# A 3x3 convolution by transformed tiles: three sums per image group on GpSimd in place of VectorE

## The chip, the cores and the metric

The kernel runs on one core of a Trainium2 chip. A core has TensorE (PE in the profile, with PEld for its weight loads), which multiplies matrices and writes to PSUM; VectorE (DVE) and ScalarE (ACT), which work element by element on SBUF and PSUM; GpSimd (POOL), which can also work element by element on SBUF and issues some of the transfers; and SyncE (SP), which here only issues transfers. Each engine runs its own queue in order, and engines wait for each other by semaphores. The metric is device time in microseconds.

## The reference

Two bottleneck layers, one after the other, on 64 images of 1024 channels, 14 x 14 pixels, all in fp32. A layer is:

```python
out = relu(_bn(_conv(x,   w1, b1, 1, 0)))     # 1x1, 1024 -> 256
out = relu(_bn(_conv(out, w2, b2, 1, 1)))     # 3x3, 256 -> 256
out =      _bn(_conv(out, w3, b3, 1, 0))      # 1x1, 256 -> 1024
x   = relu(x + softplus(residual_scale) * out)
```

The batch norm `_bn` takes mean and variance of each channel over the batch itself, so a stage has to have ended before the next can be normalised. The change lies in the 3x3 convolution, which runs once in each layer.

## The kernel before

The 256-channel activation of all 64 images, `y_all`, stays in SBUF: 128 partitions, two slots of channels (`MS` = 2), 12544 pixels. The stages are the first 1x1 convolution (to about 309 us of the profiled span), the 3x3 convolution of layer 0 (`conv2`, to about 560), the statistics and the fused third and first convolutions of the two layers (to about 1310), the 3x3 convolution of layer 1 (to about 1565) and the last stage.

`conv2` works on eight groups of eight images (`NG` = 8, `GI` = 8), in place: a group's rows in `y_all` are read, and its results are put down in the same rows. In the direction of the rows it computes four output rows from six transformed products (`NF` = 6), in the direction of the columns even and odd columns from four filters (`NK` = 4). The six products of a group come in three pairs, (1, 2), (3, 4) and (5, 0).

- **Inputs.** For each pair, VectorE forms combinations of rows (`combine`: the tiles `steps` and `r`, by `stt`, a scalar_tensor_tensor at L593, and by additions at L682, L688 and L699), then sums, differences and steps of columns (`sums` L624, `v` L630, `diffs` L640). ScalarE makes edges (L635, L636, L590, L714 to L716).
- **Products.** For each of the six, TensorE multiplies `sums` into the bank `m`, `diffs` into `l`, and `v` into the banks `columns` (two buffers). ScalarE copies `m` into `columns` ahead of the last (L758, L760) and `l`, with both signs, into `ls` in SBUF (L768). A product with 224 columns of moving data has 32 multiplications; products 3 and 4 have 168, since the last tile of rows doesn't need them.
- **Outputs.** VectorE adds `columns` and `ls` into `f` (L801), once for each product; `f` has three buffers. The generator `finish` then puts a group together. From products 1 and 2 come `a` = their sum (tile `fa`, L829) and `d` = their difference (tile `fb`, L830); from 3 and 4 `c` (tile `fc`, L835) and `e` (L836). Output rows 1 and 2 are `d` + 2`e` and `a` + 4`c` (four L593). Output row 0 is `a` + `c` (L843) plus product 0. Output row 3 is `d` + 8`e` (L593, in place in `fb`) plus product 5 (L859); the last row of an image, which has only `d` and product 5, is L860.
- **Row 0's product 0.** In groups 0 to 5 (`by_transfer`) it is added by two transfers that accumulate in SBUF, issued by GpSimd (L871). Groups 6 and 7 add it on VectorE (L846, L873, L879). Group 7 (`last_group`) also takes statistics of its rows on VectorE as it writes them.

While a group runs, ScalarE normalises the next group and takes the moments of the one before (`long_work`, `moment`, `norm`), by long instructions over 1568 elements.

The order of the program decides TensorE's order, and some of VectorE's and ScalarE's (`keep_in_program_order`). A scheduler may permute the rest of VectorE's, ScalarE's and GpSimd's instructions by its own estimates, and places the waits. GpSimd has nothing in `conv2` but the transfers of L871 and, at the end, a few instructions on two numbers each (`merge`).

Of the kernel before, what the change touches and what calls it, by code (L numbers as in the profile page):

```python
# [87 lines left out]
def bottlenecks(ctx: ExitStack, tc: tile.TileContext, x, w1s, w2s, w3s, pars, out):  # L88
    nc = tc.nc
# [466 lines left out]
    def conv2(psum, pool, b, par, aff, affine_of, stats):  # L556
# [14 lines left out]
        full = RT - 1  # L571
# [12 lines left out]
        def new(tag, tiles=RT):  # L584
            v = pool.tile([P, MS * RT * LINE], FP, tag=tag, name=tag, bufs=BUFS.get(tag, 1))
            return v[:, : MS * tiles * LINE].rearrange("p (s r l) -> p s r l", s=MS, r=tiles)
# [5 lines left out]
        def stt(to, a, by, c):  # L592
            return nc.vector.scalar_tensor_tensor(to, a, by, c, ALU.mult, ALU.add)  # L593
# [210 lines left out]
        def halves(f):  # L804

            return f.rearrange("p o r (i q c) -> p q (o r i) c", i=GI, q=2)

        def outputs(c):
            return c.add_to(new("f", c.lines // GI))

        def finish():


            for g in range(NG):
                out_rows = [y_grp[:, :, g, k::4, :] for k in range(4)]
                last_group = g == NG - 1

                by_transfer = g < NG - 2

                def stat(k, lines):  # L820
                    if last_group:
                        for o in range(MS):
                            nc.vector.bn_stats(stats[:, o, 1 + k, :], lines[o])

                ca = yield
                fa = outputs(ca)
                fb = outputs((yield))
                a, d = new("fa"), new("fb")
                nc.vector.tensor_add(a, fa, fb)  # L829
                nc.vector.tensor_sub(d, fa, fb)  # L830

                fa = outputs((yield))
                fb = outputs((yield))
                c, e = new("fc", full), fa
                nc.vector.tensor_add(c, fa, fb)  # L835
                nc.vector.tensor_sub(e, fa, fb)  # L836
                a3, d3 = (v[:, :, :full] for v in (a, d))
                for o in range(MS):
                    stt(out_rows[1][:, o, :full], e[:, o], 2.0, d3[:, o])
                    stt(out_rows[2][:, o], c[:, o], 4.0, a3[:, o])  # L840
                if by_transfer:

                    nc.vector.tensor_add(out_rows[0][:, :, :full], a3, c)  # L843
                    nc.scalar.activation(out_rows[0][:, :, full], a[:, :, full], AF.Copy)
                else:
                    nc.vector.tensor_add(a3, a3, c)  # L846
                stt(d3, e, 8.0, d3)
                if g == 0:
                    begin(out_rows[1][:, :, :full])
                if last_group:  # L850
                    for o in range(MS):
                        lines = y_grp[:, o, g, 1 : 1 + 4 * full].rearrange("p (r k) l -> p r k l", k=4)[:, :, :2]
                        for k in range(2):
                            moment(lines, idle[:, : 2 * full * LINE].rearrange("p (r k l) -> p r k l", k=2, l=LINE), o, k, g)

                fa = outputs((yield))

                end = y_grp[:, :, g, H - 1]
                nc.vector.tensor_add(out_rows[3], d3, fa[:, :, :full])  # L859
                nc.vector.tensor_add(end, d[:, :, full], fa[:, :, full])  # L860
                stat(0, [out_rows[3][:, o] for o in range(MS)])
                stat(1, [end[:, o] for o in range(MS)])
                if last_group:
                    merge()

                cb = yield
                if by_transfer:

                    f = outputs(cb)
                    for o in range(MS):  # L870
                        nc.gpsimd.dma_start(out=out_rows[0][:, o], in_=f[:, o], accum_op=ALU.add)  # L871
                    continue
                nc.vector.tensor_add(halves(a), halves(a), cb.by_columns(cb.ls))  # L873
                for j, q in enumerate((EVEN, ODD)):
                    for o in range(MS):
                        to, more = (
                            v[:, o].rearrange("p r (i q c) -> p q r i c", i=GI, q=2)[:, q] for v in (out_rows[0], a)
                        )
                        nc.vector.tensor_add(to, cb.banks[:, q, o].rearrange("p (r i c) -> p r i c", r=RT, c=WH), more)  # L879
                    stat(2 + j, [out_rows[0][:, o].rearrange("p r (i q c) -> p q r i c", i=GI, q=2)[:, q] for o in range(MS)])  # L880
            yield
# [8 lines left out]
        def begin(lines):  # L890

            mv = small.tile([P, MS, nc.vector.BN_AGGR_DIM], FP, tag="mv_first", name="mv_first")
            for o in range(MS):
                nc.vector.bn_stats(first_stats[:, o], lines[:, o])
            for o in range(MS):
                nc.vector.bn_aggr(mv[:, o, :], first_stats[:, o])
            nc.vector.tensor_scalar(center, mv[:, :, 0], -1.0, None, ALU.mult)

        def moment(y, to, o, k, g):
            act(to, y, (AF.Identity, AF.Square)[k], bias=center[:, o : o + 1], accum_out=moments[:, o, k, g : g + 1])  # L900

        def merge():

            n = GPX * (NG - 1) + 2 * full * LINE
            m = small.tile([P, MS, 2], FP, tag="m12", name="m12")
            for o in range(MS):
                nc.vector.tensor_reduce(m[:, o], moments[:, o], mybir.AxisListType.X, ALU.add)
            eng = nc.gpsimd
            eng.tensor_scalar(m, m, 1.0 / n, None, ALU.mult)
            var = small.tile([P, MS], FP, tag="m12var", name="m12var")  # L910
            eng.tensor_tensor(var, m[:, :, 0], m[:, :, 0], ALU.mult)
            eng.tensor_sub(var, m[:, :, 1], var)
            eng.tensor_sub(m[:, :, 0], m[:, :, 0], center)

            for half in range(2):
                to = stats[:, :, 0, 3 * half : 3 * half + 3]
                eng.memset(to[:, :, 0], n / 2)
                eng.tensor_copy(to[:, :, 1], m[:, :, 0])
                eng.tensor_scalar(to[:, :, 2], var, n / 2, None, ALU.mult)
# [26 lines left out]


        made, finished = items(), finish()
        next(finished)
        queue = [next(made) for i in range(3)]  # L950
# [498 lines left out]
```

## Time and profile before

| | us |
|---|---|
| median of 3 runs | 1959.82 (1959.64 to 1960.51) |
| the profiled execution, its own time | 1959.24 |
| its span in the profile | 1957.5 |
| VectorE busy in the span | 1552.4 |
| TensorE busy in the span | 1919.9 |
| GpSimd busy in the span | 532.0 |
| L843, 12 instructions, each | 0.85 |
| L859, 16 instructions, each | 0.85 |
| L860, 16 instructions, each | 0.38 |

A line of a timeline gives start and duration in us from the start of the span, engine, source line, operation, the tiles written and read, the shape, and in brackets how long the engine had idled before it and what ended that. Tile names are those of the program without buffer numbers. Durations of successive instructions of an engine overlap a little, so the time that one takes from its engine is better read from start to start. Many matmuls have one source line, L168, which is that of a helper; they are told apart by tile. In the page's first part PE is TensorE at work on matmuls, whose ends are modelled.

### The profile page before, as it was taken

The numbers are of one execution on the slowest core, as the hardware profiler recorded it, in microseconds if no ns is written. First come the engines' busy times: TensorE is split into PE (matmuls) and PEld (weight loads), VectorE is DVE, ScalarE is ACT, GpSimd is POOL, SyncE is SP. The second block draws the span as 40 slices with busy tenths as digits, with TensorE's granted clock in tenths as the row PEclk, the third lists the DMA queues.
The fourth block names the chain that finished last, engine by engine and source line by source line (L and its number), as shares of the span: only waits on it lengthen the run. The fifth ranks groups of instructions, "written<-read, shape, count | busy, mean of one in ns | idle before, by whom it ended". The sixth has DMA issues, their size and how long they took to land.

```text
span 1957.5 us, 26989 instructions
## 1 busy us (share of the span) xinstructions
PE 1919.9 (98%) x9430; PEld 1614.4 (82%) x9430; DVE 1552.4 (79%) x2491; ACT 1041.5 (53%) x2082; POOL 532.0 (27%) x638
## 2 busy tenths in 40 slices
PE   9999999999999999999999999989999999999998
PEld 5555558999997799999999999989999887555554
DVE  5778768999998667676776776699999976888786
ACT  2222214677775055555555555457777641666665
POOL 0111100000105133433433333301010051666664
PEclk9999999999999999999999999999999999999999
DMA  7766635576747634444444444257667386899997
GB/s 289 278 248 254 249 112 165 178 208 191 207 142 203 198 135 187 173 165 177 182 169 165 179 184 166 99 183 204 203 192 207 124 199 232 298 322 339 336 341 264
DMA packets 188983, 408.39 MB, mean 209 GB/s; under 512 B 24944, under 2 KB 165136, under 8 KB 172336
## 3 DMA queue, kind: packets, MB, share of 16 engines
q1 hardware_dynamic: 161728, 324.66, 48.5%
q0 software_dynamic: 21504, 30.94, 6.9%
q10 hardware_dynamic: 5616, 51.06, 6.3%
q8 instruction: 75, 1.23, 0.3%
q14 instruction: 60, 0.49, 0.1%
HBM read 263.75 MB, written 115.34 MB: 194 GB/s over the span
## 4 chain that ended last, share of the span: by engine, by line
PE 90%; DVE 7%; issue 1%; ACT 1%; DMA 1%; SPq 0%; POOL 0%; DVEq 0%
PE ay L168 17%; PE cy L168 16%; PE columns L168 13%; PE cp L168 12%; PE ap L168 10%; PE m L168 6%; PE l L168 6%; PE ax L168 4%; PE cx L168 4%; PE ps L168 1%; DVE x L466 1%; DVE ct L431 1%; DVE f L801 0%; DMA home<-y 0%; DVE ct L433 0%
## 5 line engine op out<-in xcount | busy, mean ns | idle before, releaser
L333 ACT ACTIVATE cu<-cy,scale 128x196 f32<-128x196 f32 (+1 forms) x552 | 257.7, 473 | 286.7 <-PE cy L168 279.6
L168 PE MATMUL columns<-v,ub 128*128 128x224 f32 (+1 forms) x1536 | 301.1, 337 | 0.7 <-ACT columns L760 0.7
L168 PEld LDWEIGHTS columns<-v,ub 128*128 128x128 f32 x1536 | 269.4, 188 | 4.1 <-ACT columns L760 1.2
L333 ACT ACTIVATE x<-x,shift 128x392 f32<-128x392 f32 x428 | 239.7, 613 | 55.1 <-POOL x L492 53.2
L466 DVE SCALAR_TENSOR_TENSOR x<-cp,scale,x 128x196 f32<-128x196 f32 (+1 forms) x368 | 178.1, 484 | 98.0 <-PE cp L168 96.4
L168 PE MATMUL cy<-ct,ws 128*128 128x196 f32 (+1 forms) x736 | 222.0, 383 | 1.1 <-ACT cu L333 1.1
L168 PE MATMUL ay<-at,ws 128*128 128x196 f32 (+1 forms) x752 | 209.2, 381 | 0.0
L487 POOL TENSOR_TENSOR x<-x,cu 128x196 f32<-128x196 f32 (+1 forms) x184 | 159.2, 865 | 174.1 <-ACT cu L333 162.5
L492 POOL TENSOR_TENSOR x<-x,cu 128x392 f32<-128x392 f32 x124 | 125.9, 1015 | 192.8 <-DVE x L466 188.1
L168 PEld LDWEIGHTS ay<-at,ws 128*128 128x128 f32 x752 | 136.4, 190 | 33.6 <-ACT au L333 0.5
L168 PEld LDWEIGHTS cy<-ct,ws 128*128 128x128 f32 x736 | 133.4, 190 | 36.4 <-ACT cu L333 3.8
L168 PE MATMUL m<-sums,ua 128*128 128x224 f32 (+1 forms) x752 | 147.6, 340 | 6.2 <-DVE sums L624 6.2
L168 PE MATMUL l<-diffs,ub 128*128 128x224 f32 (+1 forms) x768 | 149.7, 338 | 3.0 <-PE columns L168 2.9
L513 POOL TENSOR_TENSOR x<-x,cu 128x392 f32<-128x392 f32 x120 | 124.5, 1038 | 86.1 <-DVE x L466 79.2
L871 POOL DMA_DIRECT2D y<-f x24 | 31.1, 1532 | 412.8 <-DVE f L801 320.8
L168 PEld LDWEIGHTS l<-diffs,ub 128*128 128x128 f32 x768 | 133.6, 189 | 7.0 <-PE columns L168 5.9
L168 PEld LDWEIGHTS m<-sums,ua 128*128 128x128 f32 x752 | 132.2, 191 | 8.7 <-DVE sums L624 7.9
L466 DVE SCALAR_TENSOR_TENSOR x<-cx,scale,x 128x196 f32<-128x196 f32 (+1 forms) x184 | 89.3, 485 | 59.1 <-PE cx L168 58.2
L333 ACT ACTIVATE au<-ay 128x196 f32<-128x196 f32 (+1 forms) x141 | 53.6, 380 | 152.0 <-PE ay L168 149.3
L168 PE MATMUL cx<-y,w 128*128 128x196 f32 (+1 forms) x404 | 124.1, 392 | 0.4 <-DVE x L1130 0.4
L168 PE MATMUL cy<-y,w 128*128 128x196 f32 (+1 forms) x404 | 123.8, 392 | 0.0
L168 PE MATMUL cp<-zt 128*128 128x257 f32 x392 | 118.8, 385 | 1.8 <-DVE zt L1030 1.7
(211 smaller groups left out, 3950.1 us busy)
## 6 DMA issues: line engine op xcount, KB each, us to landing
x<-in_x SPq DMA_DIRECT2D x62, 1568.0 KB, 6.8
ub<-u SPq DMA_DIRECT2D x94, 768.0 KB, 5.0
x<-mid SPq DMA_DIRECT2D x32, 1568.0 KB, 8.6
mid<-x ACTq DMA_DIRECT2D x31, 1568.0 KB, 5.1
out<-x SPq DMA_DIRECT2D x123, 392.0 KB, 6.5
ua<-u SPq DMA_DIRECT2D x94, 256.0 KB, 3.0
u<-y POOLq DMA_DIRECT2D x48, 256.0 KB, 5.9
home<-y SPq DMA_DIRECT2D x90, 96.0 KB, 4.2
```

The lines of the kernel that those rows point to most:

```text
L168: tc.keep_in_program_order(nc.tensor.matmul(*args, **kw))
L333: tc.keep_in_program_order(nc.scalar.activation(*args, **kw))
L431: nc.vector.tensor_add(t2, t3, ys[0][0])
L466: nc.vector.scalar_tensor_tensor(v, bank, self.scale[:, o : o + 1], v, ALU.mult, ALU.add)
L487: nc.gpsimd.tensor_add(self.part(1, 1), self.part(1, 1), u3)
L492: nc.gpsimd.tensor_add(v, v, self.u12)
L513: nc.gpsimd.tensor_add(v, v, self.u12[:, i * self.n : (i + 1) * self.n])
L871: nc.gpsimd.dma_start(out=out_rows[0][:, o], in_=f[:, o], accum_op=ALU.add)
```

## The change

Three sums of `finish` are issued on GpSimd: the last step of output row 0 that isn't a transfer (`a` + `c`, groups 0 to 5), and the sum that puts down output row 3 with the last row of each image (groups 0 to 6). Group 7 keeps its sums on VectorE. Values and places are the same. In each of the two 3x3 convolutions GpSimd gets 6 + 7 + 7 instructions, which VectorE loses. From the second hunk on, line numbers of the changed kernel are higher by one: L859 and L860 become L860 and L861, L871 becomes L872.

```diff
@@ -840,7 +840,7 @@
                     stt(out_rows[2][:, o], c[:, o], 4.0, a3[:, o])
                 if by_transfer:
 
-                    nc.vector.tensor_add(out_rows[0][:, :, :full], a3, c)
+                    nc.gpsimd.tensor_add(out_rows[0][:, :, :full], a3, c)
                     nc.scalar.activation(out_rows[0][:, :, full], a[:, :, full], AF.Copy)
                 else:
                     nc.vector.tensor_add(a3, a3, c)
@@ -856,8 +856,9 @@
                 fa = outputs((yield))
 
                 end = y_grp[:, :, g, H - 1]
-                nc.vector.tensor_add(out_rows[3], d3, fa[:, :, :full])
-                nc.vector.tensor_add(end, d[:, :, full], fa[:, :, full])
+                eng = nc.vector if last_group else nc.gpsimd
+                eng.tensor_add(out_rows[3], d3, fa[:, :, :full])
+                eng.tensor_add(end, d[:, :, full], fa[:, :, full])
                 stat(0, [out_rows[3][:, o] for o in range(MS)])
                 stat(1, [end[:, o] for o in range(MS)])
                 if last_group:
```

## The prediction

> **What bounds the kernel now.** I began with the page's first two parts, to see which engines are full and where.
>
> ```profile
> span 1957.5 us, 26989 instructions
> PE 1919.9 (98%) x9430; PEld 1614.4 (82%) x9430; DVE 1552.4 (79%) x2491; ACT 1041.5 (53%) x2082; POOL 532.0 (27%) x638
> ```
>
> TensorE is busy over the whole span, but the change touches only the two 3x3 convolutions, about 309 to 559 us and 1316 to 1563 us. So I read two image groups there (columns: stretch, length, busy time and instructions of PE, PEld, DVE, ACT and POOL, then clock, DMA).
>
> ```profile
> 418.42:452.50 34.08, 33.76 (x193) 33.23 (x193) 33.43 (x37) 24.99 (x49) 2.55 (x2) 1.00 0.70 198
> 452.50:486.60 34.10, 33.77 (x192) 33.27 (x193) 33.45 (x37) 25.06 (x49) 2.56 (x2) 1.00 0.68 197
> ```
>
> Here VectorE is as full as TensorE: 33.4 of 34.1 us against 33.8. Which sets the pace is told by who waits. From 384 to 520 us, VectorE's one listed wait is for ScalarE, never for TensorE; TensorE pauses once a group.
>
> ```profile
> DVE r L593 <- ACT r L715: 1.2, 4, 0.3
> ...
> PE l L168 <- PE columns L168: 0.6, 2, 0.3
> ```
>
> ```profile
> 416.57 1.54 PE columns L168 x8
> 418.11 0.31 issue
> 418.42 1.75 PE l L168 x8
> ```
>
> The second fence is the chain that ended last. The l product reads diffs (L640), which VectorE wrote from 417.24 to 418.32 us; the product starts at 418.42. So in a group VectorE sets the pace, and TensorE follows with only 0.3 us of its own idle time. The timeline of VectorE gives what is to move, and its neighbours:
>
> ```profile
> 414.70 0.85 DVE L843 TENSOR_TENSOR y<-fa,fc 128x672 f32<-128x672 f32 x1
> 415.47 0.85 DVE L593 SCALAR_TENSOR_TENSOR fb<-f,fb 128x672 f32<-128x672 f32 x1
> 416.24 1.08 DVE L801 TENSOR_TENSOR f<-columns,ls 128x896 f32<-128x896 f32 x1
> 417.24 1.08 DVE L640 TENSOR_TENSOR diffs<-r 128x896 f32<-128x896 f32 x1
> 418.24 0.85 DVE L859 TENSOR_TENSOR y<-fb,f 128x672 f32<-128x672 f32 x1
> 419.01 0.38 DVE L860 TENSOR_TENSOR y<-fb,f 128x224 f32<-128x224 f32 x1
> 419.31 2.95 DVE L699 TENSOR_TENSOR steps<-y 128x2688 f32<-128x2688 f32 x1
> ```
>
> Instructions overlap by 0.08 us, so by start to start L843 costs 0.77 us, L859 0.77 and L860 0.30: 1.84 us a group.
>
> **What the Trainium skill says.** "SBUF — State Buffer", Who interferes with whom: a VectorE instruction with two SBUF inputs contends with a GpSimd instruction that reads SBUF, and the later one "fully blocks"; one with at most one SBUF input, outside the two-port modes, does not contend. The trace agrees, in both directions. A GpSimd add of 128x196 takes 0.60 us alone and 1.35 us behind an L418:
>
> ```profile
> 804.06 0.97 DVE L418 TENSOR_TENSOR at<-x,at 128x784 f32<-128x784 f32 x1 [1.24 <-PE ay L168]
> ```
>
> ```profile
> 802.27 0.60 POOL L487 TENSOR_TENSOR x<-x,cu 128x196 f32<-128x196 f32 x1
> ...
> 804.14 1.35 POOL L487 TENSOR_TENSOR x<-x,cu 128x196 f32<-128x196 f32 x1 [1.27 <-ACT cu L333]
> ```
>
> The page says that issue order decides who blocks, not what happens when VectorE has an unbroken queue. The timeline near 1674 us has that case:
>
> ```profile
> 1673.89 0.64 DVE L522 TENSOR_SCALAR x<-x,shift 128x392 f32<-128x392 f32 x1
> 1674.45 1.37 DVE L430 TENSOR_TENSOR ct<-y 128x392 f32<-128x392 f32 x1
> ```
>
> ```profile
> 1674.28 1.13 POOL L487 TENSOR_TENSOR x<-x,cu 128x392 f32<-128x392 f32 x1
> ```
>
> The GpSimd add arrives while L522 runs, and L430 follows L522 without a gap. The add goes first, 0.11 us over its usual 1.02, and L430 takes 1.37 us; subtractions of its shape that meet no add take 0.55. So a waiting GpSimd gets the port ahead of VectorE's next instruction. "GPSIMD Engine Reference", Performance versus the Vector engine, gives 4497 ns for a 2048-element add, an estimate of 2.2 ns an element. The trace: 0.60 us for 196 and 1.015 for 392 (L492), so 2.13 ns an element and 0.18 fixed.
>
> **The change, part by part.** Between 0.60 and 1.015 us the line gives GpSimd 1.61 us for 672 elements and 0.66 for 224; 3.9 us a group on an engine busy 2.55 of 34 would be nothing, were it not for the port.
>
> *One block.* Behind L418, which ended at 805.03, the 196-element add ended at 805.49: 0.46 us later. With 476 more elements an add ends 0.46 + 1.01 = 1.47 us after the instruction that held it up. A blocked VectorE instruction ends 0.43 us after the add (L430: 1675.83 against 1675.40), 0.12 less than its free 0.55; unblocked it would start 0.08 before its predecessor's end. So VectorE loses 1.47 - 0.12 + 0.08 = 1.43 us to a 672-element add, and 0.48 to one of 224 (with 28 more elements, 0.06).
>
> *Where they fall.* In the changed program's order, for groups 2 to 5: L835, L640, L836, four L593 (y), L593 (fb), L801, L699, L593, L801. L843's add needs L835, so it asks while L640 runs, and goes before L836: -0.77 + 1.43. L859's needs the first of these L801, so it asks in the 2.95 us of L699, and goes before the next L593: -0.77 + 1.43. L860's comes behind that L593, beside an L801, which reads PSUM: 0.48 hidden, -0.30; without that cover +0.48. Sum: 2.86 - 1.84 = +1.02 us.
>
> *Reordering.* All of TensorE's and SyncE's instructions keep their order; the scheduler permutes some of VectorE's and ScalarE's. An L801 now stands before the L593 that waited 0.30 us for L715, so that wait is covered: -0.30. L640 before L836 brings diffs early, so the pause at l goes, but the pace is VectorE's. A group: +0.72.
>
> *Other groups.* Group 1 has other neighbours (L630, L640, L699) but the same sum. In group 0 L860 has no cover, +1.50, but there VectorE idles 1.35 us for TensorE before an L801 (at 350.96), so +0.15. Group 6 moves only L859 and L860: four L880, which read PSUM, cover 1.2 us of the first; some 0.25 + 0.48 - 1.07 = -0.35. Group 7 keeps its place. A convolution: 0.15 + 5 x 0.72 - 0.35 = 3.4; two: +6.8 us.
>
> *The rest.* The two transfers of L871 stand behind L859 and L860 on GpSimd, but wait as before for the later L801 (DVE f L801), by whose end both adds are done: nothing. They landed in 6.5 us, and ScalarE reads the rows some 12 us after issue; a delay over 2.5 us would hold up its copies for L801. L801 gets a wait on GpSimd for f's buffer, 14 us after the add was ready to go: nothing. VectorE's L801, late by up to 1.9 us within a group, runs 1.5 to 4 us after TensorE has finished its banks, so the delay does not come back round.
>
> The profiled execution took 1959.24 us, 1.74 around its span; 1957.5 + 6.8 + 1.7 = 1966.0, and as the median lies 0.6 above it, 1966.6.
>
> **Rivals.**
> *Worse packing.* L860 is never covered (+0.48) and the 0.30 us wait stays: a group costs 1.50, ten of them 15, with group 0 at 0.6 and group 6 at 0: +16, 1976. For it: the adds write and read in rows of 112, and every shift of an add against VectorE breaks a cover. Against: the order puts an L801 there.
> *VectorE keeps the port.* If its next instruction wins, an add runs only beside L801 (1.0 us of cover, 0.43 left): -1.84 + 0.86 = -1.0 a group. TensorE then limits: its pause of 0.31 us, 0.33 with start-up of the stalled product, in 14 groups is worth 4.6. By the chain's own pieces its work is less still: four products of 6.08 us (m and l 1.51 each, two columns 1.53 each) and two of 4.58 (1.14, 1.14, 1.15, 1.15) make 33.5 a group, 0.55 under 34.05, which is 7.7. Between them, 1954, faster. It decides once an add costs VectorE less than half of (1.84 + 0.30), 1.07 us. Against it: L430 above; all 13 of its instructions that meet an add there take 1.37.
> *Nothing to measure.* One of the two big adds, asking later than I put it, meets an L801: 1.43 + 0.43 - 2.14 = -0.28 a group, ten of them -2.8, and groups 0 and 6 about nothing: 1957.
>
> **How the numbers follow.** Blocks as costed or somewhat less or more, about 1962 to 1972: 0.48; worse packing, 1972 to 1982: 0.20; nothing to measure, 1956 to 1962: 0.14; VectorE keeps the port: 0.18. This kernel's measurement tells 0.2%, 3.9 us. Of the first case a tenth lies within that. So faster 0.19, same 0.17, slower 0.64. The likeliest time is 1966.6, its own range 1962 to 1972. Leaving out a tenth at either end of all cases: 1954.5 to 1977.
>
> **What would show it.** Right: L836 and the L593 behind L699 near 2.2 us where 0.85 stood, GpSimd's adds stretched by the L640 and L699 before them, groups of 34.8 us, TensorE with more pauses. Wrong: VectorE's durations unchanged and adds of many microseconds (VectorE keeps the port), or groups of 33.7 us. It is also wrong if GpSimd's late adds hold L871, and through it ScalarE, or if TensorE was the pace after all, so that VectorE can lose 0.7 us a group unseen.

## The result: 0.43% slower

| | before | changed |
|---|---|---|
| median, us | 1959.82 (1958.33 to 1960.51, 5 runs) | 1968.33 (1966.97 to 1968.77, 5 runs) |
| the profiled execution, own time / span | 1959.24 / 1957.5 | 1966.97 / 1965.2 |
| first 3x3 convolution, first to last `columns` product | 282.4 | 286.1 |
| second, likewise | 281.7 | 286.4 |
| one group in the middle (L829 to the next L829) | 34.07 | 35.21 |

The ratio of the medians is 1.0043, with a 95% interval of 1.0029 to 1.0056. The two convolutions are 3.7 and 4.6 us longer, 8.3 together; the span is 7.7 longer, so all of it is there. (The text before the result put them at about 309 to 559 and 1316 to 1563 us. By the first and last `columns` product they run from 305 to 587 and from 1276 to 1557. The groups read there lie well inside, so no step depends on it.)

From here on, line numbers of the changed kernel are used for it: L860 and L861 are the former L859 and L860.

The page of the changed kernel:

```profile
span 1965.2 us, 27005 instructions
PE 1922.3 (98%) x9430; PEld 1613.6 (82%) x9430; DVE 1561.7 (79%) x2451; ACT 1040.8 (53%) x2082; POOL 646.2 (33%) x678
```

VectorE has 40 instructions less (2451 against 2491), worth 1.84 us in most groups, and is busy 9.3 us *more*. Time in which an instruction is blocked counts as busy. One group in the middle, in the columns of the prediction's table by stretches:

```profile
435.70:470.92 35.22, 34.14 (x194) 33.15 (x193) 34.45 (x34) 24.92 (x48) 10.49 (x5) 1.00 0.66 193
```

VectorE does 34 instructions where it did 37, in 34.45 us where it took 33.43. TensorE now has more idle time than VectorE: 1.1 us of 35.2. The waits from 384 to 520 us, of TensorE and of VectorE:

```profile
PE columns L168 <- ACT columns L760: 4.0, 7, 0.8
...
DVE r L593 <- ACT r L715: 1.2, 4, 0.3
```

TensorE pauses about 1 us a group for ScalarE's copies into `columns` (L760), once for 0.81 and once for 0.26 us. Both copies stand in ScalarE's queue behind an instruction that waits for VectorE: L844, which needs `fa` (L829), and L635, which needs an L593. VectorE's only listed wait is the old one, 0.3 us a group, no shorter than before. The chain that ended last runs through VectorE for most of a group (up to 424.9 us and again from 435.7 to 460.1; between them ScalarE and, from 426.6, TensorE), where it ran through TensorE before:

```profile
446.62 1.00 DVE diffs L640
447.63 2.20 DVE f L836
...
453.27 2.88 DVE steps L699
```

Where the time is lost is seen in VectorE's timeline of one group, beside GpSimd's. First VectorE:

```profile
411.33 1.08 DVE L640 TENSOR_TENSOR diffs<-r 128x896 f32<-128x896 f32 x1
412.33 2.29 DVE L836 TENSOR_TENSOR f<-f 128x672 f32<-128x672 f32 x1
...
417.99 2.94 DVE L699 TENSOR_TENSOR steps<-y 128x2688 f32<-128x2688 f32 x1
421.03 2.10 DVE L593 SCALAR_TENSOR_TENSOR r<-steps 128x672 f32<-128x672 f32 x1
423.05 1.08 DVE L801 TENSOR_TENSOR f<-columns,ls 128x896 f32<-128x896 f32 x1
```

GpSimd, the same stretch:

```profile
411.49 2.41 POOL L843 TENSOR_TENSOR y<-fa,fc 128x672 f32<-128x672 f32 x1 [20.03 <-DVE fc L835]
418.14 4.27 POOL L860 TENSOR_TENSOR y<-fb,f 128x672 f32<-128x672 f32 x1 [4.24 <-DVE f L801]
422.36 1.29 POOL L861 TENSOR_TENSOR y<-fb,f 128x224 f32<-128x224 f32 x1
```

L843's add asks 0.16 us into L640, waits for its end, and goes before L836: 2.29 us instead of 0.85. L860's asks 0.15 us into L699, waits for all of it, and goes before the next L593: 2.10 us instead of 0.85. L861's asks in that L593 and runs beside L801, which reads PSUM and isn't stretched (1.08 us). From start to start, L836 costs VectorE 1.44 us more, and L699 with the L593 behind it 1.42 more (417.99 to 423.05 is 5.06; unhindered it is 2.87 + 0.77 = 3.64).

So it goes in groups 2 to 5 of both layers. In group 1 L836 is stretched likewise (2.28 us), but row 3's add, which asks 0.16 us into an L640, does not go next:

```profile
383.29 2.95 DVE L699 TENSOR_TENSOR steps<-y 128x2688 f32<-128x2688 f32 x1
386.16 1.08 DVE L801 TENSOR_TENSOR f<-columns,ls 128x896 f32<-128x896 f32 x1
387.16 2.51 DVE L593 SCALAR_TENSOR_TENSOR r<-steps 128x672 f32<-128x672 f32 x2
```

```profile
382.45 5.27 POOL L860 TENSOR_TENSOR y<-fb,f 128x672 f32<-128x672 f32 x1 [4.24 <-DVE f L801]
```

L699 goes ahead of it unstretched, the add runs from L699's end, and the two L593 behind L801 take 2.51 us where, in the kernel before, they took 1.61:

```profile
389.11 1.61 DVE L593 SCALAR_TENSOR_TENSOR r<-steps 128x672 f32<-128x672 f32 x2
```

That costs 0.90 us in place of 1.42, and group 1 is 1.44 + 0.90 - 1.84 = 0.50 us longer (measured: 0.49).

### The profile page after: what moved, and what is told of

Its sections match the earlier page's. It is cut to its first block, busy times and chain, and to the rows that moved or that the text cites. A ratio compares the mean times of both kernels' runs of the same rounds, so it can differ in the third digit from the quotient of the medians.

```text
span 1965.2 us, 27005 instructions
## 1 busy us (share of the span) xinstructions
PE 1922.3 (98%) x9430; PEld 1613.6 (82%) x9430; DVE 1561.7 (79%) x2451; ACT 1040.8 (53%) x2082; POOL 646.2 (33%) x678
## 4 chain that ended last, share of the span: by engine, by line
PE 78%; DVE 17%; issue 3%; ACT 2%; DMA 1%; SPq 0%; DVEq 0%; POOL 0%; ACTq 0%
PE ay L168 17%; PE cy L168 16%; PE cp L168 12%; PE ap L168 10%; PE columns L168 7%; PE ax L168 4%; PE cx L168 4%; PE m L168 3%; PE l L168 2%; DVE f L801 2%; DVE f L836 1%; DVE steps L699 1%; DVE v L630 1%; PE ps L168 1%; DVE y L593 1%
## 5 line engine op out<-in xcount | busy, mean ns | idle before, releaser
L333 ACT ACTIVATE cu<-cy,scale 128x196 f32<-128x196 f32 (+1 forms) x552 | 258.0, 474 | 285.7 <-PE cy L168 279.3
L333 ACT ACTIVATE x<-x,shift 128x392 f32<-128x392 f32 x428 | 239.6, 613 | 55.8 <-POOL x L492 53.8
L333 ACT ACTIVATE au<-ay 128x196 f32<-128x196 f32 (+1 forms) x141 | 53.7, 381 | 157.2 <-PE ay L168 154.4
L843 POOL TENSOR_TENSOR y<-fa,fc 128x672 f32<-128x672 f32 x12 | 36.0, 3003 | 256.2 <-DVE fc L835 256.2
```

What stands on the lines that cost most here:

```text
L333: tc.keep_in_program_order(nc.scalar.activation(*args, **kw))
L843: nc.gpsimd.tensor_add(out_rows[0][:, :, :full], a3, c)
```

## The experiments

### Each half alone

The first has only L843's sum on GpSimd:

```diff
-                eng = nc.vector if last_group else nc.gpsimd
-                eng.tensor_add(out_rows[3], d3, fa[:, :, :full])
-                eng.tensor_add(end, d[:, :, full], fa[:, :, full])
+                nc.vector.tensor_add(out_rows[3], d3, fa[:, :, :full])
+                nc.vector.tensor_add(end, d[:, :, full], fa[:, :, full])
```

> Only row 0's sum (L843, groups 0 to 5) is on GpSimd; row 3's stay on VectorE. Theory (a waiting GpSimd add takes its turn at the shared port, and VectorE sets the pace): L836 stretched to 2.2 to 2.3 us in every group, no other VectorE instruction stretched; a group gains 1.44 and loses 0.77 us, +0.67, some 0.1 to 0.2 more for waits that the order uncovers; total 1964 to 1968. Rival (the loss comes with the permuted order, not with the adds): about as much as the order differs, so anything between 1960 and 1968, and L836 near 0.85. Rival (TensorE waits for ScalarE's copies behind the new waits of row 3): 1960.

Measured: 1965.11 us (1964.18 to 1966.80), against 1958.90 for the kernel before on that chip; ratio 1.0030 (1.0018 to 1.0041). L836 takes 2.28 us in ten of its sixteen places, groups 1 to 5 of both layers; in group 0 it takes 0.85, and groups 6 and 7 have no such add. The groups in the middle take 34.85. So the first half alone is 0.78 us a group: 1.44 - 0.77, and 0.12 because L624 now stands directly behind L688, whose result it needs, and has to wait for it (443.24 against 443.21, where instructions otherwise overlap by 0.08).

The second has only row 3 on GpSimd:

```diff
-                    nc.gpsimd.tensor_add(out_rows[0][:, :, :full], a3, c)
+                    nc.vector.tensor_add(out_rows[0][:, :, :full], a3, c)
```

> Only row 3's sums (L860, L861, groups 0 to 6) are on GpSimd; row 0's stays on VectorE. In this order an L801, which reads PSUM, follows L699 directly, so the theory (turns at the shared port, VectorE the pace) has the 672-element add run beside it: the instruction behind that L801 is stretched by 0.4 to 0.6 us, not 1.25, for 1.07 us taken off VectorE; VectorE gets below TensorE's pace and the kernel comes out faster than before, 1954 to 1958. Rival (any GpSimd add of this size costs VectorE its 1.25 to 1.44 us wherever it lands): +0.2 to 0.4 a group, 1962 to 1965. Rival (the permuted order costs): slower than before too.

Measured: 1956.01 us (1955.65 to 1956.99); ratio 0.9985 (0.9979 to 0.9992), *faster* than before. The scheduler made another order here. VectorE:

```profile
451.09 2.94 DVE L699 TENSOR_TENSOR steps<-y 128x2688 f32<-128x2688 f32 x1
453.96 1.08 DVE L801 TENSOR_TENSOR f<-columns,ls 128x896 f32<-128x896 f32 x1
454.96 2.52 DVE L593 SCALAR_TENSOR_TENSOR r<-steps 128x672 f32<-128x672 f32 x2
```

GpSimd:

```profile
451.26 4.27 POOL L860 TENSOR_TENSOR y<-fb,f 128x672 f32<-128x672 f32 x1 [26.00 <-DVE f L801]
```

The add asks in L699 as before and starts at its end, but the next instruction is an L801. That covers 1.0 us of it; the L593 behind it takes 1.29 us instead of 0.85 (0.44 more), and the following one 1.32 (0.46 more, from the 224-element add). The two L593 are the x2 row with 2.52 us. The same two sums of row 3 thus cost VectorE 0.90 us when L801 stands behind L699 and 1.42 when L593 does, against 1.07 on VectorE itself. The groups in the middle take 34.03 us, 0.04 less than before: 0.90 - 1.07, and the same 0.12 at L624, make -0.05. The rest of the gain lies in the first and last groups. A gain to TensorE's pace (33.5, below) this is not. The two halves don't add: +6.2 and -2.9 us make 3.3, and both together cost 8.5, since each makes the scheduler choose another order. In a group in the middle it is 0.78 - 0.04 = 0.74 us against 1.14: the L801 that covered row 3's add alone is gone (1.42 - 0.90), and the 0.12 at L624 is paid once, not twice.

### The same sum at another moment, and twice

L843's add is kept on GpSimd but queued behind a copy of one element of `fb`, which becomes ready only when the last L593 of the outputs has ended, so that it asks while an L801 runs:

```diff
-                    nc.gpsimd.tensor_add(out_rows[0][:, :, :full], a3, c)
...
                 stt(d3, e, 8.0, d3)
+                if by_transfer:
+                    late = pool.tile([P, 1], FP, tag="late", name="late")
+                    tc.keep_in_program_order(nc.gpsimd.tensor_copy(late, d3[:, 0, 0, :1]))
+                    tc.keep_in_program_order(nc.gpsimd.tensor_add(out_rows[0][:, :, :full], a3, c))
```

> The changed kernel, with row 0's GpSimd add held back until L593 has written fb, by a copy of one element from fb ahead of it on GpSimd's queue, so that it asks for the port at the start of an L801. Theory: L836 is back at 0.85 us, L699 behind the L801 is stretched by 0.7 to 1.0 us in its place; 0.4 to 0.7 us a group less than the changed kernel, in 10 to 12 groups 4 to 8 us: 1960 to 1964. Rival (place doesn't matter, the add costs what it lasts): 1968 to 1971, for GpSimd has one more instruction.

Measured: 1962.85 us (1962.24 to 1964.27), ratio 1.0021 (1.0012 to 1.0029); groups of 34.55. VectorE, then GpSimd:

```profile
447.66 0.85 DVE L836 TENSOR_TENSOR f<-f 128x672 f32<-128x672 f32 x1
...
451.87 3.72 DVE L699 TENSOR_TENSOR steps<-y 128x2688 f32<-128x2688 f32 x1
```

```profile
451.16 1.62 POOL L850 TENSOR_TENSOR y<-fa,fc 128x672 f32<-128x672 f32 x1
```

L836 is back at 0.85. The add runs unhindered beside L801, in 1.62 us, and what is left of it blocks L699: 3.72 instead of 2.94. The group's change against the changed kernel, 34.55 - 35.21 = -0.66, is just -1.44 + 0.78. GpSimd has the same sums as in the changed kernel, and a copy of one element more; what changed is the instruction that the sum meets, and the loss against the kernel before fell from 8.5 us to about 4.

L843's add issued twice:

```diff
                     nc.gpsimd.tensor_add(out_rows[0][:, :, :full], a3, c)
+                    nc.gpsimd.tensor_add(out_rows[0][:, :, :full], a3, c)
```

> The changed kernel with row 0's GpSimd add issued twice, one behind the other, the same values written again. Theory (each waiting add goes ahead of VectorE's next instruction): the second asks while L836 runs and goes ahead of the L593 behind it, which is stretched by 1.3 to 1.5 us; twelve times, +15 to +18 us over the changed kernel: 1983 to 1987. Rival (VectorE keeps the port when it has an unbroken queue, and what was seen at L836 is a single case): the second add waits for an L801, +0 to +5: 1968 to 1974.

Measured: 1983.77 us (1983.28 to 1984.59), ratio 1.0125 (1.0111 to 1.0139). VectorE, then GpSimd:

```profile
453.79 1.91 DVE L593 SCALAR_TENSOR_TENSOR y<-fc,fa 128x336 f32<-128x336 f32 x1
```

```profile
453.23 2.11 POOL L844 TENSOR_TENSOR y<-fa,fc 128x672 f32<-128x672 f32 x1
```

The second add blocks the L593 behind L836: 1.91 instead of 0.50. Groups take 36.63 us, 1.42 more than in the changed kernel, with nothing given back. This is the price of one 672-element block measured by itself, and it shows that VectorE has no slack in these groups.

### What in the sum blocks: its reads or its writes

All three sums left out, for the groups that have them on GpSimd:

```diff
-                    nc.gpsimd.tensor_add(out_rows[0][:, :, :full], a3, c)
...
-                eng = nc.vector if last_group else nc.gpsimd
-                eng.tensor_add(out_rows[3], d3, fa[:, :, :full])
-                eng.tensor_add(end, d[:, :, full], fa[:, :, full])
+                if last_group:
+                    nc.vector.tensor_add(out_rows[3], d3, fa[:, :, :full])
+                    nc.vector.tensor_add(end, d[:, :, full], fa[:, :, full])
```

> The changed kernel with the three moved sums left out altogether in the groups where they were on GpSimd (so rows 0 and 3 are computed only in part), the order of VectorE's instructions in the steady groups being that of the changed kernel. It shows TensorE's pace once VectorE is no longer in the way, and whether the permuted order costs anything. Theory (turns at the port cost VectorE 2.7 us a group): nothing is stretched, VectorE has 1.8 us a group to spare against before, TensorE's first to last multiplication of a convolution is 1.5 to 4 us under before; 1952 to 1956. Rival (the permuted order, with its new waits, costs): VectorE still waits for ScalarE and itself, 1960 or more.

Measured: 1947.33 us (1947.15 to 1947.48), against 1959.33; ratio 0.9939 (0.9922 to 0.9955). From 400 to 500 us:

```profile
400.00:500.00 100.00, 100.00 (x574) 99.34 (x573) 94.77 (x100) 74.77 (x145) 7.70 (x6) 1.00 0.71 203
```

TensorE is busy without a pause, and a group takes 33.51 us. VectorE's order in these groups is that of the changed kernel, so this order without the adds holds nothing up. This is TensorE's pace, and 33.5 was the estimate from the chain's pieces. VectorE's wait for L715 grows to 1.3 us and costs nothing now. The total fell below what was expected because the first group, too, is shorter: 37.7 us, where it took 40.2 and 38.9.

Then GpSimd writes the same rows with a constant and reads nothing:

```diff
-                    nc.gpsimd.tensor_add(out_rows[0][:, :, :full], a3, c)
+                    nc.gpsimd.memset(out_rows[0][:, :, :full], 0.5)
```

and likewise for `out_rows[3]` and `end`.

> The changed kernel with the three GpSimd sums replaced by GpSimd fills of the same rows with a constant (so rows 0 and 3 are not computed): the same destinations and sizes on the same engine, but nothing read. Theory (what blocks is the read port that GpSimd shares with VectorE's second input): no VectorE instruction is stretched, time that of the kernel without the sums within 3 us, 1952 to 1957. Rival (any GpSimd instruction on SBUF takes VectorE's turn, writes too): L836 or others stretched by 0.3 us or more, 1958 to 1970. Rival (GpSimd's queue and the waits on it are the cost): as the changed kernel, 1964 to 1970.

Measured: 1948.01 us (1946.96 to 1949.16), ratio 0.9942 (0.9928 to 0.9957), groups of 33.51: as if the sums were left out, and, as there, under the range expected. VectorE, then GpSimd:

```profile
415.70 0.86 DVE L593 SCALAR_TENSOR_TENSOR r<-steps 128x672 f32<-128x672 f32 x1
```

```profile
415.71 0.66 POOL L843 MEMSET y<- 128x672 f32 x1 [28.68 <-DVE steps L699]
```

The two run at the same time, and neither is stretched. The Trainium skill, "SBUF — State Buffer", Who interferes with whom, says that a VectorE instruction with two SBUF inputs contends with a GpSimd instruction "that reads SBUF, not with one that only writes it"; this run agrees (0.86 and 0.66 us side by side). One thing limits it: the memsets don't wait for their inputs, so they also start at other moments than the sums.

Row 0 alone on GpSimd, with one input in place of two:

```diff
-                    nc.gpsimd.tensor_add(out_rows[0][:, :, :full], a3, c)
+                    nc.gpsimd.tensor_copy(out_rows[0][:, :, :full], c)
```

(with row 3 on VectorE, as in the first run of this study).

> As the run with row 0's sum alone on GpSimd, but there the add of a and c is a copy of c (so a is left out of row 0): one SBUF input in place of two, in the same place, the same 672 elements and the same wait for L835. Theory (GpSimd's reads take the port; how long is up to how it reads): L836 is stretched again, but by less, for the copy reads half as much; the Trainium skill (GPSIMD Engine Reference, Engine selection) has one-input operations at roughly line rate, an estimate of 0.56 us for 672 elements at 1.2 GHz, so L836 near 1.4 us in place of 2.28, and 1957 to 1961. Rival (only a GpSimd instruction with two inputs meets VectorE): L836 at 0.85, 1953 to 1957.

Measured: 1955.42 us (1954.79 to 1956.81), against 1959.06; ratio 0.9981 (0.9974 to 0.9988). VectorE:

```profile
443.67 1.08 DVE L640 TENSOR_TENSOR diffs<-r 128x896 f32<-128x896 f32 x1
444.67 1.40 DVE L836 TENSOR_TENSOR f<-f 128x672 f32<-128x672 f32 x1
```

GpSimd:

```profile
443.82 1.54 POOL L843 COPY y<-fc 128x672 f32<-128x672 f32 x1 [20.24 <-DVE fc L835]
```

A copy of 672 elements takes 0.55 us from VectorE, where the sum takes 1.44. Most of the copy's 1.54 us is its wait in L640: it ends 0.61 us after L640, where the sum ended 1.49 after it. That is as expected, and the groups in the middle (33.97) are what it gives: 34.07 - 0.77 + 0.55 + 0.12 (L624 again). The total came out 1.6 us under the range expected, because the first group of layer 0 took 38.1 us instead of 40.2; what orders that group better stays open.

### A version that takes the sum off VectorE without GpSimd's reads

If GpSimd's reads are what VectorE pays for, the sums should go where product 0 of row 0 already goes: to transfers that accumulate in SBUF. VectorE's L593 then writes `d` + 8`e` to the rows themselves, and product 5 is added by transfer. On the kernel before:

```diff
-                stt(d3, e, 8.0, d3)
+                if last_group:
+                    stt(d3, e, 8.0, d3)
+                else:
+                    for o in range(MS):
+                        stt(out_rows[3][:, o], e[:, o], 8.0, d3[:, o])
+                    nc.scalar.activation(y_grp[:, :, g, H - 1], d[:, :, full], AF.Copy)
...
-                nc.vector.tensor_add(out_rows[3], d3, fa[:, :, :full])
-                nc.vector.tensor_add(end, d[:, :, full], fa[:, :, full])
+                if last_group:
+                    nc.vector.tensor_add(out_rows[3], d3, fa[:, :, :full])
+                    nc.vector.tensor_add(end, d[:, :, full], fa[:, :, full])
+                else:
+                    for o in range(MS):
+                        nc.gpsimd.dma_start(out=out_rows[3][:, o], in_=fa[:, o, :full], accum_op=ALU.add)
+                    nc.gpsimd.dma_start(out=end, in_=fa[:, :, full], accum_op=ALU.add)
```

> The kernel before, with row 3 put down as row 0 is: VectorE writes d + 8e straight to the output rows (two instructions of 336 in place of one of 672), ScalarE copies the last row, and three accumulating transfers issued by GpSimd add product 5 (groups 0 to 6). Nothing moves to GpSimd but the issuing of transfers. Theory: VectorE loses 1.07 us a group and gains 0.07, no turn at the port is taken, TensorE sets the pace: 1953 to 1957, no slower than with row 3's sums on GpSimd. Rival (descriptors for three more transfers a group, some 4 us of GpSimd's time, hold up row 0's transfers and with them ScalarE or f's buffers): 1958 to 1966.

Measured: 1953.81 us (1950.79 to 1954.87), ratio 0.9968 (0.9955 to 0.9981): faster than both kernels.

```profile
400.00:500.00 100.00, 100.00 (x575) 99.36 (x574) 97.36 (x106) 75.75 (x147) 19.03 (x15) 1.00 0.84 216
```

TensorE has no pause left, groups take 33.5 us, and no VectorE instruction from 384 to 520 us is stretched. DMA engines are busy 0.84 of this stretch, where it was 0.69 in the kernel before.

With row 0's `a` + `c` done in the same way as well:

```diff
-                    nc.vector.tensor_add(out_rows[0][:, :, :full], a3, c)
-                    nc.scalar.activation(out_rows[0][:, :, full], a[:, :, full], AF.Copy)
+                    nc.scalar.activation(out_rows[0], a, AF.Copy)
+                    for o in range(MS):
+                        nc.gpsimd.dma_start(out=out_rows[0][:, o, :full], in_=c[:, o], accum_op=ALU.add)
```

> Row 3 by transfers as in that run, and row 0's sum too: ScalarE copies all of a into the output rows (0.4 us before for the last row, some 1.0 for all), two more accumulating transfers add c, and L871's transfers then add product 0. VectorE loses a further 0.77 us in twelve groups. If VectorE still sets the pace in places (group 0, the groups behind it), 1948 to 1953, faster than with row 3 alone; if TensorE's pace is all that is left, 1952 to 1955; if the five to seven descriptor jobs a group on GpSimd, or row 0's second transfer waiting for the first, hold up ScalarE's moments: 1956 or more.

Measured: 1952.57 us (1949.93 to 1952.70), against 1959.06; ratio 0.9961 (0.9947 to 0.9975). That can't be told from the version before it: the groups were at TensorE's pace already (33.55 now), and the DMA engines are at 0.94.

### Who goes first: an idea that fell

In group 0 L843's add did not get its turn. VectorE of the changed kernel, then GpSimd:

```profile
336.31 1.08 DVE L682 TENSOR_TENSOR r<-steps 128x896 f32<-128x896 f32 x1
337.31 0.85 DVE L836 TENSOR_TENSOR f<-f 128x672 f32<-128x672 f32 x1
...
340.52 0.91 DVE L895 BATCH_NORM_STATS2 first_stats<-y 128x6 f32<-128x336 f32 x2
...
341.43 1.60 DVE L688 TENSOR_TENSOR r<-steps 128x896 f32<-128x896 f32 x1
```

```profile
336.62 5.46 POOL L843 TENSOR_TENSOR y<-fa,fc 128x672 f32<-128x672 f32 x1 [31.17 <-DVE fc L835]
```

It asked 0.31 us into L682, and then L836 and five L593 went past it unstretched; it ran only from L895 on, which has one input, and into L688, which took 1.60 us where it had taken 1.06. In the other groups this sum asked 0.16 to 0.23 us into the running instruction and went next. So I supposed that the moment of asking decides. Two kernels ask later: `c` is formed as `fa` times a column of ones plus `fb`, and GpSimd first overwrites that column's tile, of 192 elements or of one, with ones again. (L836 is L842 in both, and L843 is L850.)

```diff
-                nc.vector.tensor_add(c, fa, fb)
+                if by_transfer:
+                    if g == 0:
+                        tick = pool.tile([P, 192], FP, tag="tick", name="tick")
+                        nc.gpsimd.memset(tick, 1.0)
+                    stt(c, fa, tick[:, :1], fb)
+                else:
+                    nc.vector.tensor_add(c, fa, fb)
...
-                    nc.gpsimd.tensor_add(out_rows[0][:, :, :full], a3, c)
+                    tc.keep_in_program_order(nc.gpsimd.memset(tick, 1.0))
+                    tc.keep_in_program_order(nc.gpsimd.tensor_add(out_rows[0][:, :, :full], a3, c))
```

> As the changed kernel, but the sum c is formed as fa times a column of ones plus fb, and GpSimd, ahead of row 0's sum, overwrites that column's tile of 192 elements with ones again; it may do so only once c is formed. So row 0's sum is asked for some 0.25 us later than in the changed kernel, 0.4 to 0.5 us after VectorE's running instruction (the multiply-add just behind c) began, instead of 0.16 to 0.23. Theory (the moment decides: a request early in the running instruction goes next, a late one, as in group 0 at 0.31, loses to VectorE's queue): L836 takes 0.85 us in groups 1 to 6, GpSimd's sum waits for some 4 to 5 us past the unbroken queue, as in group 0 now, and costs what it meets then no more than 0.8 us; the time is 1959 to 1965 us. Rival (group 0 is special by what runs there, and the moment doesn't matter): L836, or the instruction that stands behind the request, takes 2.2 to 2.3 us, and the time is 1966 to 1971 us.

> As the run beside it, with a tile of one element, so that the request comes only some 0.1 us later than in the changed kernel, at about 0.26 to 0.32 us after the running instruction began. Theory (the moment decides): this lies between the 0.23 that went next and the 0.31 that lost, so that some groups may go one way and some the other; in each, the sides must agree with its own moment. Rival (the moment doesn't matter): L836 takes 2.28 us in all groups from 1 on, and the time is 1966 to 1971 us.

Measured: 1968.84 us (1968.21 to 1969.11) with 192, 1968.65 (1968.50 to 1968.78) with one; ratios to before 1.0050 in both (1.0033 to 1.0066 and 1.0035 to 1.0065). With 192, VectorE and GpSimd:

```profile
413.56 2.28 DVE L842 TENSOR_TENSOR f<-f 128x672 f32<-128x672 f32 x1
```

```profile
412.92 2.20 POOL L850 TENSOR_TENSOR y<-fa,fc 128x672 f32<-128x672 f32 x1
```

The add asked 0.36 us into L640, later than the one that lost in group 0, and went next all the same; group 0's asked 0.36 us into L682 in this run, and lost again. So the moment doesn't decide, and the rival was right on these groups. With the tile of one element, group 0's add asked 0.20 us into L682 and lost again in both layers; and in group 1, at the same 0.20 us into the same L630, layer 1's add went next and layer 0's lost, for 6.24 us. What decides is open. The runs show only how often: of the 36 requests of row 0's sum in the changed kernel and these two, 29 went ahead of VectorE's next instruction, and the seven that lost were the six of group 0 and this one.

Row 3's add in group 1 says the same. In four kernels it asked 0.15 or 0.16 us into the same L640, with the same L699 next. In both layers it lost in the changed kernel and with row 3 alone on GpSimd, and in both it went first with 192 elements and with row 0's sum issued twice (L699 then took 4.37 or 4.38 us). So neither the moment nor VectorE's two instructions around it decide.

## Why the prediction was right, and which steps were not

The predicted 1966.6 us lies 1.7 under the measured median of 1968.33, 0.09%, and the sign was that of the case called likeliest. Step by step:

**What bounds the kernel: right.** That VectorE sets the pace of a group is shown from both sides: the second add of 1.42 us lengthened a group by 1.42, and with the sums left out a group fell from 34.07 to 33.51, where TensorE stops it.

**The price of a block: right.** 1.43 us was worked out for a 672-element add and 0.48 for one of 224. Measured: 1.44 (L836), 1.42 (L699 with its L593), 1.42 (the add issued twice), and 0.46 for the small one in the run with row 3 alone. GpSimd's time alone, put at 1.61 us, is 1.62. (The words "fully blocks" are in the section that the prediction names for the two-port modes; for two SBUF inputs the Trainium skill, "SBUF — State Buffer", has them under Summary: rules for kernel authors. The trace agrees nearly: L836 ended 0.72 us after the add, of its free 0.85.)

**Where the adds fall: right for groups 2 to 5.** In the prediction's line numbers, L843's blocks L836, L859's blocks the L593 behind L699, L860's hides beside L801. In group 1 only L843's blocks as costed, in group 0 only row 3's two. That the L593 is the one met is a choice of the scheduler; with L801 there the block is 0.44.

**Reordering: wrong.** The step read -0.30, since an L801 now stood before the L593 that waited for L715. That wait is 0.29 still. VectorE is there at 429.78, after L801, instead of 429.69; but L715 ends only at 430.04. ScalarE of the changed kernel:

```profile
426.46 1.69 ACT L333 ACTIVATE y<-y,shift,scale 128x1568 f32<-128x1568 f32 x1
428.05 0.38 ACT L590 ACTIVATE r<-y 128x224 f32<-128x224 f32 x1
...
428.61 0.96 ACT L768 ACTIVATE ls<-l 128x448 f32<-128x448 f32 x2
429.46 0.58 ACT L715 ACTIVATE r<-steps 128x448 f32<-128x448 f32 x1
```

Before, ScalarE had idled 1.39 us for `diffs` ahead of L590. Now `diffs` is ready when ScalarE gets there, but L590 stands behind a long L333, and two L768 have come between L714 and L715, which starts 0.32 us before VectorE is free for the L593; before, it was 0.30. I had moved VectorE's instructions and left ScalarE's where they were. The other term missed here is the 0.12 us of L624 behind L688, an L801 having stood between them before. So a group in the middle is 1.44 + 1.42 - 1.84 + 0.12 = 1.14 us longer, as measured, and not 0.72; the difference is the 0.30 that wasn't hidden and this 0.12.

**Other groups.** Group 1 is 0.49 us longer (0.72 predicted), by two misses that offset each other: the 0.30 us wait stayed, and row 3's add cost 0.90 in place of 1.43.

For groups 0 and 4 one L640, 1.0 us, has to be put where it belongs: the changed kernel does it before the L829 that ends group 0, the kernel before does it after that L829 and catches up only in group 4. With it, group 4 is 1.13 us longer, like its neighbours. Group 0 is 1.07 us shorter in layer 0 and 0.25 longer in layer 1, where +0.15 was predicted for both. Its adds cost VectorE 0.54 us at L688, 1.40 at L630 and 0.46 at L640; less 1.84 that is +0.56, not the +1.50 of the prediction, since row 0's add lost its turns. In layer 0 VectorE's idle time of 1.35 us is gone too, as argued; layer 1 had no such idle time to give, and I had read it in layer 0 alone. A further 0.3 us less, in both layers, is not accounted for.

Groups 6 and 7, read together, are 0.30 and 0.37 us shorter (-0.35 predicted). TensorE is busy throughout there (568 to 588 us, in both kernels).

**The sum.** Group 0, group 1, groups 2 to 5 and the last two together: -1.07 + 0.49 + 4.55 - 0.30 = 3.67 in layer 0 and 0.25 + 0.49 + 4.27 - 0.37 = 4.64 in layer 1, where 0.15 + 0.72 + 2.88 - 0.35 = 3.40 was predicted for each. (In layer 1 one of groups 2 to 5 had taken 0.3 us longer before.) Groups 2 to 5 lose some 1.5 us more than predicted, and in layer 0 most of that is given back by group 0, for a reason that the prediction didn't have. So the total hits more closely than its terms deserve; that part is luck.

**The rest: right.** ScalarE has no wait for a transfer in its list from 384 to 520 us, and no engine but GpSimd itself waits for its late adds.

**The rivals.** VectorE keeping the port did happen, to row 0's add in group 0 and to row 3's in group 1: four of the 26 big adds of the changed kernel. Worse packing is half of what happened: the 0.30 us wait stayed, but the cover of the 224-element add (L860 there) held. Nothing to measure: the moved request that meets an L801 is the run with row 0's add asked later. It saves 0.66 us a group against the changed kernel, but is 0.48 above the kernel before, not 0.28 below: its block is 0.78 us (0.43 in the rival), the 0.30 us wait stayed, and L624 costs 0.12.

## What to carry to other kernels

A sum of two SBUF inputs handed from a full VectorE to GpSimd is no gift: here 0.77 us of work became 1.42 us of blocked time. With an instruction that reads PSUM behind the one that it waits for, the two sums of row 3, 1.07 us of work, became 0.90. Count GpSimd's duration against the VectorE instruction that follows the one it waits for, and ask for each engine, not only the one relieved, in which order its own queue now runs. Here accumulating transfers, beside which no VectorE instruction was stretched, brought the groups down to TensorE's pace (1959.33 to 1953.81 us).

## What the hardware showed beyond expectation

The Trainium skill, "SBUF — State Buffer", Who interferes with whom, says that issue order decides who blocks. In group 0 of the changed kernel that doesn't hold: row 0's add was there 0.69 us before L836 began, and L836 and five L593 went first; the add took 5.46 us. In group 1 L699 went ahead of row 3's add, which had asked 0.84 us before it began. Most requests of the same kind went next, those of row 0's sum from 0.16 to 0.37 us into the running instruction. The runs exclude the moment of asking as the reason, and leave the reason open.

How long VectorE is blocked depends on how much GpSimd reads: for 672 elements written, L836 lost 1.44 us to a sum of two inputs and 0.55 us to a copy of one, and a fill that reads nothing stretched no VectorE instruction (0.86 us for the L593 beside it).
